# Reordering the first stages of a fused cross-attention kernel

## The chip, the cores and the metric

The kernel runs on one core of one Trainium2 chip. Its engines work side by side, each through a queue of its own in the order of the program: TensorE (PE, matrix products, with PEld for the loading of its weights), VectorE (DVE), ScalarE (ACT), GpSimd (POOL) and SyncE (SP), whose queue issues nearly all transfers (DMAs). The metric is the device time of one execution in microseconds (us), lower is better. Everything is computed in float32.

## The reference

Eight batches of 112 rows `x` with 320 channels attend to contexts of 375 rows with 512 features. The last 4 context rows are "prompts"; the other 371 are text. There are 20 heads of 16 channels.

```python
q   = heads(hidden_states @ W_q)
k_t = heads(text_ehs @ W_k)
v_t = heads(text_ehs @ W_v)
probs_t  = softmax(einsum('bhsd,bhtd->bhst', q, k_t) * attn_scale)
text_out = einsum('bhst,bhtd->bhsd', probs_t, v_t)
k_ip, v_ip = heads(ip_ehs @ W_k_ip), heads(ip_ehs @ W_v_ip)
attn_scores = einsum('bhsd,bhnd->bhsn', q, k_ip) * attn_scale
qsem = l2norm(einsum('bhst,bte->bhse', probs_t, text_ehs))
sem  = einsum('bhse,bne->bhsn', qsem, l2norm(ip_ehs))
probs_ip = softmax(attn_scores + 0.5 * sem) * spatial_mask
out = (text_out + einsum('bhsn,bhnd->bhsd', probs_ip, v_ip)) @ W_out + b_out + hidden_states
```

## The kernel before

**The scheme.** The norm of `qsem` is taken without forming it: with the gram matrix G of the text rows, the squared norm is the sum of p (G p) over the text. Per batch the kernel builds a wide matrix `u`: the upper triangle of the gram (its diagonal blocks halved and everything doubled), the products of the text with the normalised prompts, a column of ones, and 16 value columns. One product of the turned, unnormalised probabilities with `u` then gives, for each head, the row for the norm, the prompts' similarities, the sum of the softmax and the text output (line 770, tile `ps_qd`).

**Staging.** A batch has 5 groups of 4 heads. The main loop runs over steps (batch, group). A step multiplies its group by `u` in 12 blocks of 32 text rows, computes scores, maxima (VectorE, line 721) and exponentials (ScalarE, line 735) of the group two steps ahead (`LEAD = 2`), sends these probabilities by DMA into a tile `xg` (line 742), where VectorE turns them (line 751, `turned`), and at its end runs pieces of the next batches' preparation (`between`): gram, values, keys, queries, and the turning of the context of the batch after next on VectorE (line 428, three pieces a batch). The order of PE, VectorE, SP and, in the loop, ScalarE is the order of the program text; the first stages, up to `prologue.close()`, are in program order on every engine.

**The first stages** (lines 1157 to 1203). Batch 0's context comes in three chunks of up to 128 rows, turned by PE (`transposed_context`, line 438) and copied out by ScalarE (first and third chunk) and VectorE (second). `awake(n)` multiplies the identity by itself to keep PE busy. `first_gram` yields after each of six products (line 476): chunk 1 by itself, chunks 1 and 2 with chunk 2, all three with chunk 3. `normalised_prompts` scales the prompts (square root on ScalarE, line 278) and turns both the scaled and the unscaled ones on PE (line 288). ScalarE doubles the gram into `ug` (line 492), GpSimd halves the diagonal blocks (line 493). `gram_to_groups` (line 538) copies `ug` into `u` by DMA: 4 blocks of 32 rows, each to 4 groups of 32 partitions, 16 transfers. Then follow queries (line 369, three chunks; scaled by VectorE, line 378, and copied by ScalarE, line 382), keys (line 562), the scores of the first two groups, values (line 596), and their regrouping and placing into `u` (lines 616 and 668). `spread` (line 143) rearranges columns of the weights on GpSimd.

**Banks.** PE's outputs outside the main product and the scores rotate through two banks (`ps_mm`, from `bank()`); the scores rotate through two others (`ps_sc`), which `bank(..., spare=True)` takes as well. A product waits until the bank's last contents have been read.

**Loads.** SP issues in program order: batch 0's context, a part of `x`, the weights of queries, keys and values, batch 1's context; then `ug` to `u` and the probabilities as they come; behind the first stages the two prompt weights (`load_embed`), and at the end of the first step the whole of batch 2's context (`load_next`, eight transfers). In steps, `run(("c", nb + 1), ...)` turns one third of the next context but one: for batch 2 at groups 1 and 2 of batch 0 and in group 4.

Of the kernel before, what the change touches and what calls it, by code (L numbers as in the profile page):

```python
# [8 lines left out]
F32 = mybir.dt.float32  # L9
AF = mybir.ActivationFunctionType  # L10
ALU = mybir.AluOpType
# [9 lines left out]
def kernel(  # L21
# [14 lines left out]
    nc = tc.nc  # L36
# [131 lines left out]
            )  # L168

    def load_ctx(b):  # L170
        if b > 0:
            load_ctx_blocks(b)
            return loaded[b]
        ct = io.tile([P, NT, E], F32, tag="ct", name=f"ct_{b}")
        for c in range(NT):
            rows = min(P, T - c * P)
            some = rows - rows % 16
            nc.sync.dma_start(ct[:some, c, :], ehs[b, c * P : c * P + some, :])
            if some < rows:
                nc.sync.dma_start(ct[some:rows, c, :], ehs[b, c * P + some : c * P + rows, :])  # L180
        return ct
# [13 lines left out]
    load_pairs(nc.sync, wq_sb, w_q)  # L195
    load_embed(nc.sync, wk_sb, w_k)
    load_embed(nc.sync, wv_in, w_v)
    loaded[1] = load_ctx(1)
    load_x_blocks(1, 0)

    half = const.tile([P, NT, P], F32, tag="half", name="half")
# [65 lines left out]

    def normalised_prompts():

        sq = work.tile([N, E], F32, tag="ipn", name="ipsq", bufs=1)  # L270
        ss = small.tile([N, 1], F32, tag="ipss", name="ipss", bufs=1)
        nc.vector.tensor_tensor_reduce(
            out=sq, in0=ip_sb, in1=ip_sb, scale=1.0, scalar=0.0, op0=ALU.mult, op1=ALU.add,
            accum_out=ss,
        )
        nc.vector.tensor_scalar_max(ss, ss, EPS * EPS)
        rn = small.tile([N, 1], F32, tag="iprn", name="iprn", bufs=1)
        nc.scalar.activation(rn, ss, AF.Sqrt)
        nc.vector.reciprocal(rn, rn)

        ipn = work.tile([N, E], F32, tag="ipn", name="ipn", bufs=1)
        nc.vector.tensor_scalar(ipn, ip_sb, rn, 0.5, op0=ALU.mult, op1=ALU.mult)
        yield

        for src, dst, n in ((ipn, ipnT, "n"), (ip_sb, ipT, "r")):
            ps = bank(f"ps_ipT{n}")
            for e in range(NE):
                nc.tensor.transpose(
                    ps[:, e * N : (e + 1) * N], chunk(src, e), ident[:N, :N]
                )  # L290
            nc.vector.tensor_copy(
                dst, ps[:, : NE * N].rearrange("p (e n) -> p e n", n=N)
            )
        yield

    def prompt_projections():
# [87 lines left out]


    st = {}

    def load_next(b):
        if 2 <= b < B:
            loaded[b] = load_ctx(b)  # L390

    def begin(b):
        s = st[b] = dict(ct=loaded.pop(b))
# [140 lines left out]
    def gram_to_groups(b, blocks, eng=nc.sync, parts=range(GROUP)):  # L534

        for q in blocks:
            for a in parts:
# [2 lines left out]
                    ug[q * RG : (q + 1) * RG, :],  # L540
                )

    def keys(b):
        s = st[b]
        if b > 0:
            nc.gpsimd.tensor_copy(s["kT"][:, :, TT:], kip[:, :, b * NIP : (b + 1) * NIP])
        for i in range(NC):
            ps = bank(f"ps_k_{b}_{i}", spare=0 < b < B - 1 and i == FULL)
            if 0 < b < B - 1 and i == FULL:

                for c in range(NT):
                    rows = min(P, TT - c * P)
                    nc.tensor.transpose(  # L553
                        ps[:, c * P : c * P + rows],
                        s["k3"][:rows, c].rearrange("p a r d -> p (a r d)"),
                        ident[:rows, :rows],
                    )
                nc.scalar.copy(s["kT"][:, i, :TT], ps[:, :TT])
                yield
                return  # L560
            for e in range(NE):
                nc.tensor.matmul(  # L562
                    ps[:, :TT],
                    wk_sb[:, e, i * P : (i + 1) * P],
                    s["ctxT"][:, e, :TT],
                    start=(e == 0),
                    stop=(e == NE - 1),
                )
            nc.scalar.copy(s["kT"][:, i, :TT], ps[:, :TT])
            yield  # L570
# [537 lines left out]
    def between(b, g):  # L1108
# [28 lines left out]
        if g == 3:  # L1137
# [3 lines left out]
                run(("f", b - 1), None)  # L1141
            for bs in rest:
                run(("q", bs[0]), None)
        if nb + 1 < B and g in ((1, 2) if b == 0 else (0, 1, 2)):
            run(("c", nb + 1), lambda: transposed_context(nb + 1))
        for bs in first:
            if g in ((0, 1) if b == 0 else (2, 3)[: len(bs)]):
# [10 lines left out]
    prompts = normalised_prompts()  # L1158
    context = transposed_context(0)
    products = first_gram()  # L1160
    next(prompts)
    awake(4)
    next(context)
    awake(3)
    next(context)
    next(products)
    next(prompts)
    next(context)
    run(("q", 0), lambda: project_queries(pairs[0]))
    drain(products)  # L1170
    nc.scalar.preload_act_table(AF.Exp)
    gram_to_groups(0, range(QN // 2))
    run(("q", 0), None)
    order_values()
    run(("k", 0), lambda: keys(0))
# [1 line left out]
    for a in range(GROUP):  # L1177
        scores(0, 0, a, early=True)
        probabilities(0, 0, a)
    gram_to_groups(0, range(QN // 2, QN))  # L1180
    spread(nc.gpsimd, wq_sb)
    nc.gpsimd.tensor_copy(wv_sb[:, :, C:], wk_sb[:, :, FULL * P : C])
    spread(nc.gpsimd, wk_sb)
# [2 lines left out]
    for a in range(GROUP):  # L1186
        scores(0, 1, a, early=True)
        probabilities(0, 1, a)
    run(("v", 0), None)
    drain(turned(0, 0, BLK))  # L1190
    for some in ([(a, a) for a in range(GROUP)], *across[1:]):
        regrouped(0, nc.gpsimd.tensor_copy, some)
    regrouped(0, nc.scalar.copy, across[0])
    placed(0, 0)
    run(("k", 0), None)
    run(("q", 0), None)
    load_x_blocks(2, 1)
    load_embed(nc.sync, wkip_sb, w_k_ip)
    load_embed(nc.sync, wvip_sb, w_v_ip)
    run(("k", 0), None)  # L1200
    run(("v", 1), lambda: values(1))
    more_constants()
# [36 lines left out]
    for n, (b, g) in enumerate(steps[:-NG]):  # L1239
# [11 lines left out]
        for j, _ in enumerate(multiplied(b, g)):  # L1251
            if j == 0:
# [10 lines left out]
                    probabilities(*c, a, hold=True)  # L1263
                if n == NG - 1:
                    run(("c", LEAD), None)
            if j == 5:
                for c, a in then:
                    scores(*c, a)
# [28 lines left out]
        if g == 0 and b > 1:  # L1297
            run(("f", b - 2), None)
        load_rest(n)
        if n == 0:  # L1300
            load_next(2)
        if g in ctx_blocks and b < B - 3:
            load_ctx_blocks(b + 3, ctx_blocks[g])
        for c, i in x_loads.get((b, g), ())[1:]:
# [162 lines left out]
```

## Time and profile before

| | |
|---|---|
| median of 3 runs | 416.43 us (415.19 to 416.9) |
| the profiled execution | 415.67 us, of which 414.0 us are the span of its instructions |
| busy: PE / VectorE / ScalarE / GpSimd | 98% / 82% / 52% / 31% of the span |
| granted TensorE clock, mean | 1.00 |
| start of the first main product | 35.4 us |
| DMA, share of 16 engines | 51.6% for the main queue |

In rows of instructions in order of time the first number is the start in us from the start of the span, the second the time to the end of the last of the group, and `xN` the number of instructions put together; in square brackets stands how long the engine was idle before and what ended that. One float32 product of a chunk is two passes on PE. In the list of waits the columns are: total us, times, longest. In the chain of waits each row is one piece of the chain that ended last.

### The profile page before, as it was taken

What the parts mean: (1) busy time and instruction counts of PE and PEld (TensorE: products, weight loads), DVE (VectorE), ACT (ScalarE), POOL (GpSimd) and SP (SyncE); (2) the same over time, 40 slices, a digit from 0 to 9 for tenths busy, and PEclk for the clock granted to TensorE, in tenths of its full rate; (3) what the DMA queues carried; (4) which work ended last, traced back from release to release, by engine and by line L of the source; (5) the groups of instructions that cost most, each with busy time, mean ns of one, the idle gap of its engine ahead of it and who ended that gap; (6) DMA issues with size and microseconds to landing.
All of it is one profiled execution on the core that took longest, in us unless ns stands there. A gap on an engine that the chain in (4) does not pass through costs nothing.

```text
span 414.0 us, 14122 instructions
## 1 busy us (share of the span) xinstructions
PE 406.8 (98%) x5490; PEld 319.8 (77%) x5490; DVE 338.0 (82%) x731; ACT 217.0 (52%) x729; POOL 126.7 (31%) x314
## 2 busy tenths in 40 slices
PE   8999999999999999999999999999999999999995
PEld 7766778797777867788677877788777987787893
DVE  4455489988899979889799988888798977889784
ACT  2543234636365453745357363653637563688773
POOL 5442121112081212612054120702117120545540
PEclk9999999999999999999999999999999999999999
DMA  6766856556655455455554555546444356544300
GB/s 186 193 164 177 191 142 154 154 149 163 176 143 149 140 144 142 107 144 167 129 138 127 145 150 137 152 107 180 123 126 114 96 169 159 129 123 132 108 2 29
DMA packets 46723, 57.56 MB, mean 139 GB/s; under 512 B 9501, under 2 KB 41057, under 8 KB 46656
## 3 DMA queue, kind: packets, MB, share of 16 engines
q1 hardware_dynamic: 46616, 56.60, 51.6%
q8 instruction: 43, 0.70, 0.7%
q14 instruction: 24, 0.20, 0.2%
q10 hardware_dynamic: 40, 0.07, 0.1%
HBM read 15.88 MB, written 1.39 MB: 42 GB/s over the span
## 4 chain that ended last, share of the span: by engine, by line
PE 93%; DVE 3%; DMA 2%; ACT 1%; issue 0%; SPq 0%; DVEq 0%
PE ps_qd L770 41%; PE ps_v L596 14%; PE ps_s L699 11%; PE ps_k L562 10%; PE ps_g L520 7%; PE ps_q L369 3%; PE ps_o L987 3%; PE ps_g L476 1%; DMA ct<-in_ctx_dram 1%; DVE xgT L751 1%; DMA xg<-p 1%; PE ps_k L578 1%; PE ps_k L553 1%; ACT p L735 1%; PE ps_a L975 0%
## 5 line engine op out<-in xcount | busy, mean ns | idle before, releaser
L770 PE MATMUL ps_qd<-u,xgT 32*112 32x168 f32 (+11 forms) x3840 | 217.2, 350 | 0.0
L770 PEld LDWEIGHTS ps_qd<-u,xgT 32*112 32x112 f32 x3840 | 185.6, 172 | 25.1 <-issue 0.7
L751 DVE STREAM_TRANSPOSE xgT<-xg 128x512 f32<-128x512 f32 (+2 forms) x79 | 125.9, 1601 | 7.1 <-DMA xg<-p 5.1
L735 ACT ACTIVATE p<-ps_s,nmx 112x371 f32<-112x371 f32 x156 | 84.5, 579 | 86.7 <-DVE nmx L721 81.6
L721 DVE TENSOR_REDUCE nmx<-ps_s 112x1 f32<-112x371 f32 x160 | 78.4, 535 | 26.8 <-PE ps_s L699 22.0
L816 DVE CUSTOM_DVE_ANT_0 junk<-ps_qd,p 112x371 f32<-112x371 f32 x146 | 79.2, 543 | 19.8 <-ACT pvs L783 4.2
L668 POOL COPY u<-vr 128x64 f32<-128x64 f32 x120 | 26.5, 239 | 134.3 <-PE ps_qd L770 102.2
L699 PE MATMUL ps_s<-kT,qm 32*112 32x375 f32 (+1 forms) x320 | 65.9, 495 | 0.0
L596 PE MATMUL ps_v<-wv_sb,ctxT 128*128 128x384 f32 (+1 forms) x192 | 63.3, 479 | 0.8 <-ACT qT L382 0.8
L596 PEld LDWEIGHTS ps_v<-wv_sb,ctxT 128*128 128x128 f32 x192 | 35.6, 190 | 23.1 <-ACT qT L382 1.4
L562 PE MATMUL ps_k<-ctxT,wk_sb 128*128 128x371 f32 x136 | 46.7, 486 | 0.0
L699 PEld LDWEIGHTS ps_s<-kT,qm 32*112 32x112 f32 x320 | 25.8, 171 | 12.2 <-issue 10.2
L616 ACT COPY vr<-vext 32x240 f32<-32x240 f32 x88 | 34.2, 389 | 1.3
L562 PEld LDWEIGHTS ps_k<-ctxT,wk_sb 128*128 128x128 f32 x136 | 24.5, 189 | 13.4
L603 ACT COPY vext<-ps_v 128x384 f32<-128x384 f32 (+1 forms) x24 | 11.2, 467 | 39.7 <-PE ps_v L596 39.7
L520 PE MATMUL ps_g<-ctxT 128*32 128x375 f32 (+11 forms) x672 | 30.4, 333 | 0.0
L520 PEld LDWEIGHTS ps_g<-ctxT 128*32 128x32 f32 x672 | 27.7, 110 | 2.0
L737 ACT COPY ipl<-ps_s 112x4 f32<-112x4 f32 x140 | 23.1, 165 | 0.0
L428 DVE STREAM_TRANSPOSE ctxT<-ct 128x512 f32<-128x512 f32 x21 | 23.0, 1106 | 0.0
L962 POOL TENSOR_TENSOR wv<-vip,w 112x1280 f32<-112x1280 f32 x6 | 14.8, 2468 | 26.7 <-DVE w L899 26.7
L492 ACT ACTIVATE ug<-ps_g 128x375 f32<-128x375 f32 (+2 forms) x24 | 8.3, 375 | 25.5 <-issue 12.0
L493 POOL TENSOR_TENSOR ug<-ug,half 128x128 f32<-128x128 f32 (+1 forms) x24 | 10.5, 449 | 29.2 <-ACT ug L492 29.2
(169 smaller groups left out, 337.4 us busy)
## 6 DMA issues: line engine op xcount, KB each, us to landing
xg<-p SPq DMA_DIRECT2D x156, 162.3 KB
u<-ug SPq DMA_DIRECT2D x128, 99.0 KB
ct<-in_ctx_dram SPq DMA_DIRECT2D x28, 176.0 KB
vip<-vipd SPq DMA_DIRECT2D x6, 560.0 KB
xr_sb<-in_x_dram SPq DMA_DIRECT2D x32, 35.0 KB
out_dram<-ob SPq DMA_DIRECT2D x8, 140.0 KB
x_sb<-in_x_dram SPq DMA_DIRECT2D x6, 140.0 KB
xg<-wv_sb SPq DMA_DIRECT2D x4, 162.3 KB
```

Source lines behind the costliest of these rows:

```text
L520: nc.tensor.matmul(ps[c][q * RG : (q + 1) * RG, j * RG - c * P : T - c * P], ctxT[:, e, j * RG : (j + 1) * RG], ctxT[:, e, j * RG : T], st ...
L562: nc.tensor.matmul(ps[:, :TT], wk_sb[:, e, i * P : (i + 1) * P], s["ctxT"][:, e, :TT], start=(e == 0), stop=(e == NE - 1),)
L596: nc.tensor.matmul(ps[:, :w], ctxT[:, e, c * P : (c + 1) * P], wv_sb[:, e, :w], start=(e == 0), stop=(e == NE - 1),)
L616: copy(s["vr"][a * RG : (a + 1) * RG, q::QN].rearrange("p c g d -> p c (g d)"), s["vext"][q * RG : (q + 1) * RG, :, a * w : (a + 1) * w],)
L668: nc.gpsimd.tensor_copy(v, dealt(b, c, s["vr"][:, c * QN : (c + 1) * QN, g, :]))
L699: nc.tensor.matmul(ps[:S, :w], qm[a * RG : (a + 1) * RG, i, r, j * S : (j + 1) * S], s["kT"][a * RG : (a + 1) * RG, i, :w], start=True, st ...
L721: nc.vector.tensor_reduce(nmx, s["sc", g, a][:S, :TT], AX.X, ALU.max, negate=True)
L735: nc.scalar.activation(s["p", g][:, a, :], ps[:S, :TT], AF.Exp, bias=nmx)
L737: nc.scalar.copy(s["ipl"][:, groups[g][a], :], ps[:S, TT:T])
L751: nc.vector.transpose(xT[:, j0:j1].rearrange("p j (k q) -> p q j k", q=QN), xg[:, :, j0 * RG : j1 * RG].rearrange("p q (j k) -> p q j k", ...
L770: nc.tensor.matmul(banks[a][:S, j * RG : UW], xT[a * RG : (a + 1) * RG, j, :S], region(b, c)[a * RG : (a + 1) * RG, q, j * RG - c * P :], ...
L816: nc.vector.tensor_tensor_reduce(out=junk, in0=ps[:S, :TT], in1=s["p", g][:, a, :], scale=1.0, scalar=0.0, op0=ALU.mult, op1=ALU.add, accu ...
```

## The change

- The first gram piece comes ahead of the second context chunk's turn, the third chunk right after the second, and 2 instead of 3 identity products ahead of them.
- The prompts are turned once, by a product with a 32 x 64 matrix: the identity beside a diagonal of 0.5 over the norm. It gives unscaled and scaled prompts in one bank. The scaling is moved from the 32 x 512 prompts to the 32 x 32 diagonal.
- `grams_in_place`: GpSimd copies, for each block q, the rows that stay on the same partitions (32 x 792). By DMA go the other 12 of 16: block 0 to three groups first, the nine others after the first group's probabilities.
- The third query chunk goes ahead of the second and third key chunks, and ahead of the turn of the first group's probabilities.
- The prompts' value weights are loaded in the first step instead of ahead of it. Batch 2's context is loaded in two halves, at the ends of the first and second step, and its turns are at groups 2 and 3 instead of 1 and 2 (the last in group 4 as before).
- Batch 1's third key chunk takes a bank of `ps_mm` instead of `ps_sc`.

```diff
@@ first stages: loads
-    loaded[1] = load_ctx(1)
+    load_ctx_blocks(1)
@@ def normalised_prompts():
+        both = small.tile([N, 2 * N], F32, tag="ipid", name="ipid", bufs=1)
+        nc.vector.tensor_copy(both[:, :N], ident[:N, :N])
...
-        ipn = work.tile([N, E], F32, tag="ipn", name="ipn", bufs=1)
-        nc.vector.tensor_scalar(ipn, ip_sb, rn, 0.5, op0=ALU.mult, op1=ALU.mult)
-        yield
-
-        for src, dst, n in ((ipn, ipnT, "n"), (ip_sb, ipT, "r")):
-            ps = bank(f"ps_ipT{n}")
-            for e in range(NE):
-                nc.tensor.transpose(
-                    ps[:, e * N : (e + 1) * N], chunk(src, e), ident[:N, :N]
-                )
-            nc.vector.tensor_copy(
-                dst, ps[:, : NE * N].rearrange("p (e n) -> p e n", n=N)
-            )
+        nc.vector.tensor_scalar(both[:, N:], ident[:N, :N], rn, 0.5, op0=ALU.mult, op1=ALU.mult)
+        yield
+
+        ps = bank("ps_ipT")
+        for e in range(NE):
+            nc.tensor.matmul(
+                ps[:, e * 2 * N : (e + 1) * 2 * N], chunk(ip_sb, e), both, start=True, stop=True
+            )
+        v = ps[:, : NE * 2 * N].rearrange("p (e k n) -> p k e n", k=2, n=N)
+        nc.vector.tensor_copy(ipnT, v[:, 1])
+        nc.vector.tensor_copy(ipT, v[:, 0])
         yield
@@
+    def grams_in_place(b):
+
+        for q in range(QN):
+            some = slice(q * RG, (q + 1) * RG)
+            nc.gpsimd.tensor_copy(st[b]["u"][some, q * GW : (q + 1) * GW], ug[some, :])
+
@@ def keys(b):
-            ps = bank(f"ps_k_{b}_{i}", spare=0 < b < B - 1 and i == FULL)
+            ps = bank(f"ps_k_{b}_{i}", spare=1 < b < B - 1 and i == FULL)
@@ def between(b, g):
-        if nb + 1 < B and g in ((1, 2) if b == 0 else (0, 1, 2)):
+        if nb + 1 < B and g in ((2, 3) if b == 0 else (0, 1, 2)):
@@ the first stages
-    next(prompts)
     awake(4)
     next(context)
-    awake(3)
+    next(prompts)
+    awake(2)
+    next(products)
     next(context)
-    next(products)
+    next(context)
     next(prompts)
-    next(context)
     run(("q", 0), lambda: project_queries(pairs[0]))
     drain(products)
     nc.scalar.preload_act_table(AF.Exp)
-    gram_to_groups(0, range(QN // 2))
+    grams_in_place(0)
+    gram_to_groups(0, (0,), parts=range(1, GROUP))
...
-    gram_to_groups(0, range(QN // 2, QN))
+    for q in range(1, QN):
+        gram_to_groups(0, (q,), parts=[a for a in range(GROUP) if a != q])
...
     run(("v", 0), None)
+    run(("q", 0), None)
     drain(turned(0, 0, BLK))
...
     run(("k", 0), None)
-    run(("q", 0), None)
     load_x_blocks(2, 1)
     load_embed(nc.sync, wkip_sb, w_k_ip)
-    load_embed(nc.sync, wvip_sb, w_v_ip)
@@ the main loop
+            if n == 0 and j == 2:
+                load_embed(nc.sync, wvip_sb, w_v_ip)
...
-        if n == 0:
-            load_next(2)
+        if n < 2:
+            load_ctx_blocks(2, halves[n])
```

More of the change, by code (lines that the diff above doesn't have):

```diff
@@ L386 @@
     st = {}
-    def load_next(b):
-        if 2 <= b < B:
-            loaded[b] = load_ctx(b)
     def begin(b):
```

3 lines of the change are left out of this document (removed).

## The prediction

> **What bounds the kernel now.** I read the page's engine table first, then the list of TensorE's waits, then the instructions in order of time for the stages that the change touches.
>
> ```profile
> PE 406.8 (98%) x5490; PEld 319.8 (77%) x5490; DVE 338.0 (82%) x731; ACT 217.0 (52%) x729; POOL 126.7 (31%) x314
> ```
>
> TensorE (PE) is busy for 406.8 of 414.0 us. Where it has work it is the bound, so an edit gains only what it takes from PE's work or PE's waits. This is the whole list of waits of 0.5 us or more:
>
> ```profile
> PE ps_w L455 <- POOL ident masks.py:199: 1.5, 1, 1.5
> PE ps_v L596 <- ACT qT L382: 0.8, 1, 0.8
> PE ps_wT L1074 <- DVE w_last L1069: 0.8, 1, 0.8
> PE ps_k L553 <- ACT ipl L737: 0.5, 1, 0.5
> ```
>
> The first and third lie outside the change. It touches the second (0.8 us, at the first chunk of batch 1's values) and the fourth (0.5 us, at batch 1's third key chunk). With the work before the first gram, that is all there is to win. Gains in transfers that arrive earlier behind a busy PE count nothing.
>
> **The change part by part.** (a) *The opening.* PE in order of time:
>
> ```profile
> 1.47 2.08 PE L455 MATMUL ps_w<-ident 128*128 128x128 f32 x8 [1.47 <-POOL ident masks.py:199]
> 3.56 1.13 PE L438 MATMUL ps_c<-ident,ct 128*128 128x128 f32 x4
> 4.48 0.89 PE L455 MATMUL ps_w<-ident 128*128 128x128 f32 x6
> 5.54 0.75 PE L438 MATMUL ps_c<-ident,ct 128*128 128x128 f32 x4 [0.17 <-DMA ct<-in_ctx_dram]
> 6.21 1.16 PE L476 MATMUL ps_g<-ctxT 128*128 128x128 f32 x8
> 7.30 0.66 PE L288 MATMUL ps_ipTn<-ident,ipn 32*128 32x32 f32 x4
> 7.81 0.64 PE L288 MATMUL ps_ipTr<-ident,ip_sb 32*128 32x32 f32 x4
> 8.38 0.74 PE L438 MATMUL ps_c<-ident,ct 115*128 115x115 f32 x4
> 8.95 4.63 PE L476 MATMUL ps_g<-ctxT 128*128 128x128 f32 x40
> 13.42 0.83 PE L369 MATMUL ps_q<-xT,wq_sb 128*128 128x112 f32 x6
> ```
>
> Start to start, the costs are 0.67 us for the second chunk's turn, 1.09 for the first gram piece, 0.51 + 0.57 for the prompts' two turns, 0.57 for the third chunk, 4.47 for the other 40 passes. From 5.54 PE never rests, so the queries start at 13.42. The six idle-filling passes at 4.48 become four, and the first gram piece goes ahead of the second chunk, into time in which PE now waits for data. It needs the first chunk copied out by ScalarE:
>
> ```profile
> 2.14 1.28 ACT L278 ACT_TABLE_LOAD   x1 [2.14 <-issue]
> 5.60 0.56 ACT L448 COPY ctxT<-ps_c 128x512 f32<-128x512 f32 x1
> 5.73 0.15 DVE L279 RECIPROCAL iprn<-iprn 32x1 f32<-32x1 f32 x1 [0.27 <-ACT iprn L278]
> 6.32 0.69 DVE L446 COPY ctxT<-ps_c 128x512 f32<-128x512 f32 x1
> ```
>
> Today that copy stands behind the square root of the prompts. Afterwards it comes first, as soon as the turn that started at 3.56 ends (4.69): done at 5.25, and the gram piece starts at about 5.3. Then: second chunk 6.4, third 7.1, ready for the prompts at 7.65. The program's order shows a price: a second table load of ScalarE between copy and square root, 1.28 us: 5.25 + 1.28 = 6.5, root and reciprocal and one small VectorE operation to about 7.1, still early enough. But the prompts' product takes the bank of the second chunk, which VectorE frees 0.69 us after about 7.2: 7.9, a wait of 0.25. The product has eight passes; at 4.47/40 = 0.11 each that is 0.9, against 1.08 for the two turns. No row shows this form: the bounds are 0.45 (half the passes of the gram at its pace) and 1.08 (eight at the 0.135 of the old turns); 0.9, the gram's pace, is nearest in kind. End: 7.9 + 0.9 + 4.47 = 13.3, against 13.42. **Gain 0.1** (bounds: 0.6 gained, 0.1 lost).
>
> (b) *Some of the first grams' rows by GpSimd.* Of 16 DMAs u<-ug 4 become GpSimd copies; of the rest three instead of eight stand ahead of the first probabilities on SP. Rows of the stage:
>
> ```profile
> 15.27 0.40 POOL L1182 COPY wv_sb<-wk_sb 128x256 f32<-128x256 f32 x1
> 17.68 5.09 SPq L538 DMA_DIRECT2D u<-ug  x8
> 22.86 3.72 SPq L742 DMA_DIRECT2D xg<-p  x4
> 23.19 0.20 POOL L505 COPY ctxT<-ipnT 128x16 f32<-128x16 f32 x1 [6.11 <-DVE ctxT L428]
> 25.75 2.66 PE L562 MATMUL ps_k<-ctxT,wk_sb 128*128 128x371 f32 x8
> 26.05 0.44 ACT L603 COPY vext<-ps_v 128x320 f32<-128x320 f32 x1
> 28.24 0.82 PE L369 MATMUL ps_q<-xT,wq_sb 128*128 128x112 f32 x6
> 29.05 1.17 PE L562 MATMUL ps_k<-ctxT,wk_sb 128*128 128x371 f32 x3
> 29.17 2.95 DVE L751 STREAM_TRANSPOSE xgT<-xg 128x1536 f32<-128x1536 f32 x1 [3.63 <-DMA xg<-p]
> 31.96 0.28 DVE L378 TENSOR_SCALAR qm<-ps_q,emask 128x112 f32<-128x112 f32 x1
> 32.27 0.25 ACT L382 COPY qT<-ps_q 128x112 f32<-128x112 f32 x1 [3.36 <-DVE qm L378]
> 32.58 2.85 PE L596 MATMUL ps_v<-wv_sb,ctxT 128*128 128x384 f32 x8 [0.79 <-ACT qT L382]
> 33.67 0.58 POOL L668 COPY u<-vr 128x64 f32<-128x64 f32 x3 [2.08 <-DMA u<-ug]
> ```
>
> An issue of u<-ug takes 5.09/8 = 0.64 us, so the probabilities leave SP at about 19.6 instead of 22.86, and the last u<-ug is out by 19.6 + 3.72 + 9 x 0.64 = 29.1 instead of 26.58 + 8 x 0.64 = 31.7. The transfer's 3.63 us and most of the 2.08 us of GpSimd's wait go, but PE works on keys meanwhile: worth nothing by itself. Price on GpSimd: 4 copies of 792 columns; at most 0.40 x 792/256 = 1.24 each, together 5.0, against its 6.11 us of idle before 23.19. The spreading of the weights' columns behind them is wanted by the queries' third chunk only (28.24, afterwards about 25.6) and is done by some 22. **Cost 0**; without that cover it would hold PE by what it exceeds.
>
> (c) *Queries ahead of keys.* Today the third query chunk's scaling (31.96) stands on VectorE behind the turn (29.17, 2.95 us), ScalarE's copy waits for it, and PE's first value chunk of batch 1 waits for their bank: 0.79 us. Afterwards the queries come right after the last values, and the scaling stands ahead of the turn. PE: 25.65 queries, 26.45 key chunk 1 (whose bank ScalarE frees at 26.05 + 0.44 = 26.49 today, hence no or 0.05 us of waiting), 28.95 key chunk 2, 31.45 values. Banks: key chunk 2 wants the query bank, free by some 27; values want that of key chunk 1, copied out by about 29.6. So the 0.79 goes. The ends of passes are modelled: key chunk 1 takes 28.24 - 25.75 = 2.49 from start to start, and the second's first pass at 29.05 + 2.49 is 31.54, by which the stall was 1.04. **Gain 0.9**, between the two. Late next is GpSimd's placing (33.67): in the new order done by 32, PE wants it at about 34.2.
>
> (d) *Second half of batch 2's context one group later, its turns at groups 2 and 3, batch 1's third key chunk in another bank.* Two kinds of load move past each other on SP: four of the eight context loads go behind group 1's probabilities, the prompts' value weights behind two probability transfers. SP is ahead by then (b), and no row shows PE waiting for these. But VectorE's turn of 1.05 us moves from group 1 to group 3, ahead of the maxima of batch 1's second group. The chain of waits there, with two rows of the engines:
>
> ```profile
> 76.30 0.81 DVE L378 TENSOR_SCALAR qm<-ps_q,emask 128x224 f32<-128x224 f32 x2 [0.25 <-PE ps_q L369]
> 78.10 1.05 DVE ctxT L428
> 79.14 1.25 DVE xgT L751
> 81.44 0.57 ACT p L735
> 82.12 0.54 PE ps_k L553 x3
> 82.73 0.54 ACT L558 COPY kT<-ps_k 128x371 f32<-128x371 f32 x1
> 83.81 0.51 PE ps_ip L678 x6
> ```
>
> VectorE is without a gap from 76.30 to past 82, so the extra 1.05 moves everything behind it. The exponentials come at 82.5, and ScalarE's copy of the key chunk, third behind them in its queue, at 83.8 to 84.3. The 0.5 us wait before the key chunk goes (its bank is no longer one of the scores'), but the new bank is one of two that rotate: key chunk, queries, prompt logits. The logits need the bank of the key chunk, so they wait for that copy: 84.3 instead of 83.81. **Loss 0.5** in place of the gain of 0.5; bounds: gain 0.5, loss 1.05. At the next step VectorE has idle time and the delay runs out.
>
> Sum: -0.1 - 0.9 + 0.5 = -0.5 us. The profiled execution took 415.67 us (span 414.0 and 1.67 around it): 415.2. The median of the runs, 416.43, lies 0.76 above it; by the median I forecast **415.9 us**.
>
> [...] One microsecond of the opening by windows (PE, weight loads, VectorE, ScalarE, GpSimd, clock):
>
> ```profile
> 2.00:3.00 1.00, 1.00 (x7) 1.00 (x6) 0.97 (x2) 0.86 (x1) 0.94 (x5) 1.00 0.86 266
> ```
>
> The passes of the identity at 1.47 cost 2.08/8 = 0.26 each, those at 4.48 0.89/6 = 0.15: PE became fast by 4.5, before the passes that are removed. [...]
>
> **The rivals.** *A: VectorE's move costs nothing*, if the loads or PE's lead leave it room in group 3: both waits go, -0.1 - 0.9 - 0.5 = -1.5: 414.9. Against it: the only idle time in the row is 0.25. *B: slower.* VectorE's 1.05 is not made up in the next step; the second pair of scores there waits for exponentials as well and PE loses up to 1.05 once more: +0.55, 417.0. It decides once the delay left at that point passes some 0.1 us more than PE's own 0.5. *C: slow clock in the opening.* The first gram piece runs at 0.26/0.15 of its price: 1.09 becomes 1.9, and the sum -0.5 + 0.8 = +0.3: 416.7. *D: the query bank is not the wait.* If another bank or the earlier stage takes the 0.9, what stays is -0.1 + 0.5: 416.8.
>
> **How the numbers follow.** Forecast 0.45, A 0.29, B 0.13, C 0.05, D 0.08. About 0.5% (2.1 us) is what a measurement of this kernel can tell from no change: its three runs spread by 1.7 us. All five cases lie within it; with that spread and the bounds (at best -0.6 - 1.04 - 0.5 = -2.1; at worst, with D and the bound of (d), 0.1 + 1.05 = +1.15) I give faster 0.15, same 0.77, slower 0.08. The range 414.4 to 417.2 takes in A and B with part of the runs' spread.
>
> **What the next profile would show.** (a) the first gram piece at about 5.3, a second table load behind ScalarE's first copy, the queries at 13.3; if later than 13.5, (a) is wrong. (b) first probabilities issued from about 19.6; GpSimd's four copies done before 20. (c) no wait of PE before batch 1's first values, which start near 31.4. (d) no wait at the third key chunk, one of about 1 us at the prompt logits for ScalarE's key copy; if the logits don't wait, A holds. Wrong altogether if PE's list shows a wait of over 0.5 us anywhere else: for a context load in group 2, or at the second scores of group 4.

## The result and the profile after

The changed kernel takes **417.13 us** (median of 22 runs, 416.49 to 419.69), the kernel before 415.99 us in 22 runs of the same comparison (414.71 to 417.3). The ratio is 1.0042 with a 95% interval of 1.0026 to 1.0057: slower by 0.4%, where 0.1% faster was forecast (415.9 us). It lies inside the bound of 0.5% and at the upper end of the range (417.2), but on the other side of the kernel before than was forecast.

One thing is needed to read the median: the executions of the changed kernel fall into two groups, 14 of the 22 at 416.49 to 417.24 us and 8 at 418.63 to 419.69. The kernel before has no such gap. The profiled execution, 417.11 us with a span of 415.4, is of the lower group.

The engine table of the changed kernel, and its list of TensorE's waits:

```profile
PE 408.4 (98%) x5488; PEld 319.8 (77%) x5488; DVE 340.5 (82%) x732; ACT 218.5 (53%) x730; POOL 129.7 (31%) x318
```

```profile
PE ps_w L448 <- POOL ident masks.py:199: 1.5, 1, 1.5
PE ps_wT L1073 <- DVE w_last L1068: 1.1, 1, 1.1
PE ps_ip L677 <- ACT kT L557: 0.5, 1, 0.5
PE ps_ipT L285 <- DVE ctxT L439: 0.3, 1, 0.3
```

PE is busy for 1.6 us more with two instructions fewer. The two waits that the change touches (0.8 and 0.5) are gone, one of 0.5 at the prompt logits is new, and so is one of 0.3 ahead of the prompts' product. More busy time without more work points at passes that have become slower. PE in order of time, in the opening and at the first scores of the main loop:

```profile
5.34 1.39 PE L469 MATMUL ps_g<-ctxT 128*128 128x128 f32 x8
...
7.99 2.08 PE L285 MATMUL ps_ipT<-ipid,ip_sb 32*128 32x64 f32 x8 [0.32 <-DVE ctxT L439]
9.99 4.72 PE L469 MATMUL ps_g<-ctxT 128*128 128x128 f32 x40
14.55 0.83 PE L366 MATMUL ps_q<-xT,wq_sb 128*128 128x112 f32 x6
...
32.77 2.74 PE L595 MATMUL ps_v<-wv_sb,ctxT 128*128 128x384 f32 x8
35.45 0.57 PE L698 MATMUL ps_s<-kT,qm 32*112 32x371 f32 x2
...
84.17 0.76 PE L677 MATMUL ps_ip<-kipb,qT 128*112 128x32 f32 x6 [0.54 <-ACT kT L557]
84.86 0.57 PE L698 MATMUL ps_s<-kT,qm 32*112 32x375 f32 x2
```

The same two points in the kernel before, main loop's start and batch 1's start:

```profile
35.36 0.57 PE L699 MATMUL ps_s<-kT,qm 32*112 32x371 f32 x2
...
84.24 0.57 PE L699 MATMUL ps_s<-kT,qm 32*112 32x375 f32 x2
```

Read as a ledger, the time goes like this. The first queries start 1.13 us later than before (14.55 against 13.42): that is the opening, and most of it is the prompts' product, 2.00 us from start to start for eight passes, 0.25 each, where the two turns took 1.08. How large this difference is depends on the execution. PE's first passes follow each other at 0.21 us, until they become fast (0.11). In the kernel before the queries start at 13.42 where that comes at 4.6 us, as in this profile, and at 14.28 where it comes at 7.7 ("The queries alone" below). The changed opening gains nothing by an early moment: 14.55 at 5.9 us here, and 14.57 at 4.8 in the run with batch 2's context as before. So the 1.13 is that of an early execution, and in late ones it may be less. The main loop begins only 0.09 later (35.45 against 35.36), so the queries ahead of the keys won 1.04 us. At the start of batch 1 the delay is 0.62 (84.86 against 84.24): the wait for ScalarE's key copy and what goes with it cost 0.53. Another 0.2 comes in the step after that (below), and the last 0.5 in the tail, where one small VectorE operation on PE's path took 0.65 us in place of 0.18. VectorE in the tail of the changed kernel, and below it of the kernel before:

```profile
401.05 0.65 DVE L870 TENSOR_TENSOR rn<-ss,z 112x16 f32<-112x16 f32 x1 [0.15 <-ACT shared L808]
```

```profile
400.22 0.18 DVE L871 TENSOR_TENSOR rn<-ss,z 112x16 f32<-112x16 f32 x1
```

This operation isn't touched by the change. In a second profile of the same kernel (the repeat, below) the wait that follows it is 0.8 us, as before, so it belongs to single executions; what causes it stayed open. Without it the sum is 0.1 + 0.5 + 0.2 = 0.8 us, and the middle run of the lower group, 416.77, lies 0.8 above the median of before. That the two agree so well is in part luck, as the opening of the one profile of before is an early one.

What the forecast saw and did not see of VectorE's move, in rows of VectorE, ScalarE and the weight loads of the changed kernel:

```profile
77.01 1.08 DVE L421 STREAM_TRANSPOSE ctxT<-ct 128x512 f32<-128x512 f32 x1
...
82.29 0.57 ACT L734 ACTIVATE p<-ps_s,nmx 112x371 f32<-112x371 f32 x1 [0.97 <-DVE nmx L720]
83.58 0.54 ACT L557 COPY kT<-ps_k 128x371 f32<-128x371 f32 x1
...
85.55 0.27 PEld L769 LDWEIGHTS ps_qd<-u,xgT 32*112 32x112 f32 x2 [0.40 <-DVE ss L815]
```

and the weight loads of the kernel before at the same place:

```profile
84.71 0.43 PEld L770 LDWEIGHTS ps_qd<-u,xgT 32*112 32x112 f32 x2 [0.18 <-DVE ss L816]
```

The turn runs at 77.01, ScalarE's exponentials wait 0.97 us for the maxima behind it, the key copy follows at 83.58, and the prompt logits wait for it. Besides, the next step's products need banks that VectorE's reductions (`ss`) free, and these come later too: 0.40 us at the first block where it was 0.18.

### The profile page after: what moved, and what is told of

It reads as the page before. It is cut to its first block, busy times and chain, and to the rows that moved or that the text cites. A ratio compares the mean times of both kernels' runs of the same rounds, so it can differ in the third digit from the quotient of the medians.

```text
span 415.4 us, 14117 instructions
## 1 busy us (share of the span) xinstructions
PE 408.4 (98%) x5488; PEld 319.8 (77%) x5488; DVE 340.5 (82%) x732; ACT 218.5 (53%) x730; POOL 129.7 (31%) x318
## 4 chain that ended last, share of the span: by engine, by line
PE 93%; DVE 4%; ACT 1%; issue 1%; POOL 0%; DVEq 0%; POOLq 0%
PE ps_qd L769 39%; PE ps_v L595 15%; PE ps_k L561 11%; PE ps_s L698 10%; PE ps_g L513 7%; PE ps_q L366 3%; PE ps_o L986 3%; PE ps_g L469 1%; DVE junk L815 1%; PE ps_k L577 1%; PE ps_ipT L285 1%; PE ps_w L448 0%; PE ps_a L974 0%; PE ps_k L552 0%; DVE nmx L720 0%
```

## The experiments

Two theories of the slow product stood at the start. The first goes by its weights: `chunk(ip_sb, e)` takes every fourth element of a row, so neighbours in the weights are 16 bytes apart, and reading them is slow. The second (K) goes by the clock: PE's clock falls, because two identity passes and their place were given up. Beside these stood the parts (c) and (d) of the prediction, each to be tried alone. The repeats and the comparisons each have their own runs of the kernel before beside them.

**The prompts turned twice, as before.** In the changed kernel `normalised_prompts` gets its old body back; all else stays.

```diff
-        both = small.tile([N, 2 * N], F32, tag="ipid", name="ipid", bufs=1)
...
-                ps[:, e * 2 * N : (e + 1) * 2 * N], chunk(ip_sb, e), both, start=True, stop=True
+        for src, dst, n in ((ipn, ipnT, "n"), (ip_sb, ipT, "r")):
+            ps = bank(f"ps_ipT{n}")
+            for e in range(NE):
+                nc.tensor.transpose(ps[:, e * N : (e + 1) * N], chunk(src, e), ident[:N, :N])
```

> The changed kernel with one thing undone: the prompts are scaled and turned twice on PE as in the kernel before, at the new place. In the changed kernel the single product took 2.08 us for its eight passes (7.99 to 9.99, 0.25 each) where I had priced 0.9. Theory F (the form of the product is slow, whatever the clock): the two turns cost about 1.1 us as before, the queries start at about 13.6 instead of 14.55, and the whole is about 1.0 us faster than the changed kernel, level with the kernel before or up to 0.3 us faster. Theory K (PE's clock is slow there because fewer identity products ran ahead): the turns take about 2 us too and nothing is gained.

Measured: 416.43 us (416.08 to 417.15, 11 runs) against 416.19 before, ratio 1.0 [0.9988, 1.0012]; no second group. PE in order of time:

```profile
8.30 0.66 PE L285 MATMUL ps_ipTn<-ident,ipn 32*128 32x32 f32 x4 [0.71 <-DVE ctxT L439]
8.80 0.64 PE L285 MATMUL ps_ipTr<-ident,ip_sb 32*128 32x32 f32 x4
9.37 4.72 PE L469 MATMUL ps_g<-ctxT 128*128 128x128 f32 x40
13.93 0.83 PE L366 MATMUL ps_q<-xT,wq_sb 128*128 128x112 f32 x6
```

The two turns take 1.07 us in place of 2.00, and the queries start 0.62 earlier than in the changed kernel. The other 0.3 goes into a longer wait for the bank (0.71 against 0.32), since the scaling of 32 x 512 prompts again stands on VectorE ahead of the copy that frees it. So the one product is what made the opening longer, but undoing it alone doesn't bring the opening of before back. The median is 0.7 us under that of the changed kernel, where 1.0 was expected.

**The same product with its weights side by side.** GpSimd copies the prompts into a tile in which each chunk's columns are neighbours.

```diff
+        ipc = small.tile([N, NE, P], F32, tag="ipc", name="ipc", bufs=1)
+        nc.gpsimd.tensor_copy(ipc, ip_sb.rearrange("t (p e) -> t e p", e=NE))
...
-                ps[:, e * 2 * N : (e + 1) * 2 * N], chunk(ip_sb, e), both, start=True, stop=True
+                ps[:, e * 2 * N : (e + 1) * 2 * N], ipc[:, e, :], both, start=True, stop=True
```

> The changed kernel, with the prompts first copied by GpSimd into an order in which the 128 weights of a pass lie side by side (in the changed kernel they lie 16 bytes apart); the product itself is the same. Theory F1 (the stride of the weights makes the passes slow): the eight passes take about 0.9 us, 0.11 each, and the queries start about 1.1 us earlier than 14.55. Theory F2 (a 32-row product of this kind is slow in itself): 0.25 a pass as before, no gain. Theory K (clock): no gain either.

Measured: 416.21 us (415.68 to 417.2, 12 runs), ratio 0.9995 [0.9983, 1.0008]; no second group. The product's line in three kernels, as the view of one line gives it (shortest / median / longest in ns). The kernel before, whose turns read the same strided rows:

```profile
L288 PEld LDWEIGHTS ps_ipTr<-ident,ip_sb x4: 214/214/214, 7.8 to 8.1; 32*128 32x128 f32 x4
```

the changed kernel:

```profile
L285 PEld LDWEIGHTS ps_ipT<-ipid,ip_sb x8: 303/324/327, 8.0 to 9.6; 32*128 32x128 f32 x8
```

and with the weights side by side, the line and its place in time:

```profile
L287 PEld LDWEIGHTS ps_ipT<-ipid,ipc x8: 181/187/187, 8.2 to 9.0; 32*128 32x128 f32 x8
```

```profile
8.25 1.07 PE L287 MATMUL ps_ipT<-ipid,ipc 32*128 32x64 f32 x8 [0.41 <-POOL ct L156]
13.81 0.83 PE L368 MATMUL ps_q<-xT,wq_sb 128*128 128x112 f32 x6
```

The same eight passes load their weights in 187 ns in place of 324 and take 1.0 us in place of 2.0. The moving operand, the count and the place are the same, so the layout of the weights is the cause. The queries come 0.74 us earlier than in the changed kernel, not the 1.1 expected: in this execution PE becomes fast at 6.2 us in place of 5.9, and the product starts 0.26 later (8.25 against 7.99). Its wait is named after a GpSimd operation that ends at 8.11; VectorE's copy of the second chunk, which frees the bank, ends at 8.10.

That the two turns load the same strided rows in 214 ns, where the product takes 324, no run here takes apart.

**The product issued twice.** The same result, computed once more into the same bank, to price a pass and to see what the clock does. (Of the 22 executions of the changed kernel 8 are long, not the 7 that the expectation counts.)

```diff
-            for e in range(NE):
+            for e in (*range(NE), *range(NE)):
```

> The changed kernel with the prompts' product (weights 16 bytes apart) issued twice, with the same result: 16 passes instead of 8. It measures two things. The price of a pass: 0.25 us each by the trace, so 2.0 us more. And a second effect: of 22 executions of the changed kernel 7 took 418.6 to 419.7 us and the others 416.5 to 417.3, as did 5 of 12 of the kernel with the context loads put back, but none of 23 with the prompts turned twice or with weights side by side. Theory Q (slow passes leave PE so little busy that its clock falls back for some microseconds, depending on when they come): with 4 us of them most or all executions pay the 2 us as well: about 421 us. Rival (the two groups come from something else): one third at about 421, two thirds at 419.

Measured: 421.08 us (420.48 to 422.84, 5 runs) against 415.88 before, ratio 1.0136 [1.0113, 1.0158]. PE in time, and windows of one microsecond (window, length, busy time and count of PE, weight loads, VectorE, ScalarE and GpSimd, granted clock, DMA share, GB/s):

```profile
8.25 3.99 PE L285 MATMUL ps_ipT<-ipid,ip_sb 32*128 32x64 f32 x16 [0.32 <-DVE ctxT L439]
12.17 6.86 PE L469 MATMUL ps_g<-ctxT 128*128 128x128 f32 x40
18.87 0.83 PE L366 MATMUL ps_q<-xT,wq_sb 128*128 128x112 f32 x6
```

```profile
9.00:10.00 1.00, 1.00 (x6) 1.00 (x6) 0.00 (x0) 0.00 (x0) 0.00 (x0) 0.92 1.00 379
10.00:11.00 1.00, 1.00 (x6) 1.00 (x5) 0.00 (x0) 0.00 (x0) 0.00 (x0) 0.50 1.07 410
...
13.00:14.00 1.00, 1.00 (x6) 1.00 (x6) 0.41 (x2) 0.00 (x0) 1.00 (x1) 0.50 1.19 234
...
16.00:17.00 1.00, 1.00 (x8) 1.00 (x8) 0.00 (x0) 0.00 (x0) 0.00 (x0) 0.66 0.33 74
17.00:18.00 1.00, 1.00 (x12) 1.00 (x11) 0.00 (x0) 0.48 (x1) 0.15 (x1) 1.00 0.34 60
```

Eight more passes cost 1.9 us of their own. They cost the same at a granted clock of 0.92 as at 0.50 (six in a microsecond), and each still loads its weights in 325 ns. But the run lost 5.2 us against before, where the 0.8 of the changed kernel's lower group and these 1.9 make 2.7: the clock fell to 0.50 at 9.85 us (0.92 in the window from 9 to 10), while PE was working through the slow passes without a gap, came back within the window from 16 to 17 (0.66), and the 40 passes of the gram took 6.70 us from start to start (4.56 in the changed kernel). These 2.1 us are most of the rest. In the windows, a gram pass at 13 to 14 takes twice what it takes at 17 to 18 (6 against 12 in a microsecond). The reason that theory Q gives, a PE that is little busy, no run shows: in these windows, from 9 us on, its busy share is 1.00.

**More identity passes.** K says that the clock should hold with more of them.

```diff
-    awake(2)
+    awake(4)
```

> The changed kernel with four identity products instead of two between the first chunk's turn and the first gram piece. Theory K of the rivals (fewer identity products leave the clock low for longer): the first gram piece and the product run faster, and the whole gains 0.5 us or more over 417.1. Theory F1 (the stride costs the passes their time): no gain; the first gram piece starts up to 0.5 us later, and the whole is the same or up to 0.5 us slower.

Measured: 418.57 us (417.12 to 420.3, 6 runs), ratio 1.0064 [1.0041, 1.0088]. PE in time, and one window:

```profile
6.23 1.56 PE L469 MATMUL ps_g<-ctxT 128*128 128x128 f32 x8
9.05 2.12 PE L285 MATMUL ps_ipT<-ipid,ip_sb 32*128 32x64 f32 x8 [0.32 <-DVE ctxT L439]
11.11 6.15 PE L469 MATMUL ps_g<-ctxT 128*128 128x128 f32 x40
17.09 0.83 PE L366 MATMUL ps_q<-xT,wq_sb 128*128 128x112 f32 x6
```

```profile
12.00:13.00 1.00, 1.00 (x7) 1.00 (x7) 0.35 (x2) 0.00 (x0) 1.00 (x1) 0.50 1.16 239
```

K falls: with four more passes (the first gram piece comes 0.9 us later) the product is as slow as it was, and the clock fell to 0.50 all the same, at 10.70 (0.85 in the window from 10 to 11), before the product's end. The median is 1.4 us above that of the changed kernel, more than either theory gave: 0.9 for the passes, and long executions on top. This profiled execution, 419.66 us, lies where the changed kernel's second group lies, though 0.9 of it are the extra passes. Its gram takes 5.98 us in place of 4.56, so what the fall of the clock is seen to cost is 1.4 us of the 2.4 between the groups.

No profile of the changed kernel itself fell into its second group, so that the fall of the clock makes that group is an inference from four things. They are this profile, the one of the doubled product, the absence of the group in the two kernels above that lack the slow passes (0 of 11 and 0 of 12 runs), and the mean granted clock, which is on record for every run. In the three series with the product issued once as the change has it (the changed kernel, its repeat, and the next kernel below) 15 of the 18 long runs show 0.992 to 0.995 and three 0.996; none of the 26 short ones shows less than 0.996. In the short one that was profiled, what is missing to 1.000 comes after PE's last pass, which ends at 411.8 us: from 412 on the clock reads 0.50. Two comparisons below speak against taking a fall of the clock behind slow passes for the only way to a long execution. Kernels without slow passes were long too: two of 12 runs of one (420.04 and 422.06, at 0.993 and 0.989), and one of 12 of another (418.54, at 0.999).

Why only some executions are long, no trace shows. In both profiles with a fall it came 3.4 us after PE's passes had become fast (6.43 and 9.85; 7.29 and 10.70), and lasted 6.8 and 3.4 us. In that stretch the only gap of PE in either list of waits is the one of 0.32 us ahead of the product. Where the passes became fast at 4.8, 5.9 and 6.1 us, the slow product was followed by no fall (granted clock 1.00 from 8 to 16 us). That a late start of the fast passes brings the fall about is a guess of the author from these five profiles. Turns and a wait ahead of the product do not do it by themselves: the kernel with weights side by side became fast at 6.2 us, had 1.5 us of them (6.74 to 8.25) and no slow gram behind them (4.56 us), and the doubled product had 1.4. A late start of the fast passes also moves the product itself, to 8.25 us at 6.43, which may be a part of the other 1.0 us of the second group.

**Batch 2's context as before.** Part (d) undone, the key chunk's new bank kept.

```diff
-        if n < 2:
-            load_ctx_blocks(2, halves[n])
+        if n == 0:
+            load_ctx_blocks(2)
...
-        if nb + 1 < B and g in ((2, 3) if b == 0 else (0, 1, 2)):
+        if nb + 1 < B and g in ((1, 2) if b == 0 else (0, 1, 2)):
```

> The changed kernel with batch 2's context loaded at the end of the first step and turned at groups 1 and 2 as in the kernel before; the third key chunk of batch 1 keeps its new bank. Theory of the prediction (VectorE's turn of 1.05 us, moved into group 3, delays the exponentials and the key copy): the prompt logits' wait of 0.5 us goes, batch 1's first main product starts at about 84.2 instead of 84.9, and the step behind it gains another 0.2: 0.6 to 0.9 us faster than the changed kernel. Rival (the bank alone makes the logits wait): the wait stays and the time is the same. Rival (loads in one piece hold up a turn of probabilities): a new wait in groups 1 or 2.

Measured: 416.01 us (415.63 to 418.07, 12 runs), ratio 1.0004 [0.9987, 1.0021]; the two groups are there (7 runs up to 416.06, 5 from 417.61), as the slow product is. PE in time:

```profile
83.31 0.76 PE L677 MATMUL ps_ip<-kipb,qT 128*112 128x32 f32 x6
84.00 0.57 PE L698 MATMUL ps_s<-kT,qm 32*112 32x375 f32 x2
```

The logits no longer wait, nor does the key chunk, and batch 1 starts at 84.00 in place of 84.86. So the new bank does remove the old wait, and the move of the context's turn is what puts one in its place. The lower group, 415.84 in the middle, is 0.9 us below that of the changed kernel, at the upper end of what was expected. The move costs nothing more behind batch 1's start: the next step begins at 94.36 here and at 95.23 in the changed kernel, 0.87 apart where it was 0.86. But the gain of the new bank does not last. Against the kernel before, batch 1 starts 0.24 earlier (84.00 for 84.24) and the next step only 0.03 (94.36 for 94.39), since the first blocks wait 0.40 us for VectorE's reductions here too, against 0.18 before. PE comes there earlier, VectorE doesn't.

**The queries alone.** The kernel before with one line moved.

```diff
     run(("v", 0), None)
+    run(("q", 0), None)
     drain(turned(0, 0, BLK))
...
     run(("k", 0), None)
-    run(("q", 0), None)
```

> The kernel before with one part of the change: the third query chunk ahead of the second and third key chunks. Theory of the prediction: the wait of 0.79 us before batch 1's first values goes; the first main product starts 0.8 to 1.0 us earlier than 35.4 and the whole is that much faster than the kernel before (ratio about 0.998). Rival (the transfer of the probabilities or of the grams' rows, which this kernel leaves late, takes the wait's place): the placing of values in u, at 33.7 in the kernel before, holds the first main product, and the gain is under 0.5 us.

Measured: 415.51 us (414.66 to 418.54, 12 runs) against 416.19, ratio 0.9982 [0.9965, 0.9998]. PE in time:

```profile
4.54 1.49 PE L455 MATMUL ps_w<-ident 128*128 128x128 f32 x6
14.28 0.83 PE L369 MATMUL ps_q<-xT,wq_sb 128*128 128x112 f32 x6
35.17 0.57 PE L699 MATMUL ps_s<-kT,qm 32*112 32x371 f32 x2
```

The wait of 0.79 is gone. From the first queries to the first scores it is 20.89 us, as in the changed kernel (35.45 - 14.55 = 20.90), against 21.94 before: 1.05 us won, and (b) is not in this kernel. Of this the medians show 0.7. The profile tells where the rest can go: the opening is here the code of before, yet its identity passes at 4.54 cost 0.25 each where the profile of before has 0.15, and the queries start 0.86 later. PE's passes become fast at 7.7 us here and at 4.6 there. The opening has a spread of nearly 1 us from one execution to another, by that moment.

**The mended kernel.** Prompts side by side (with a bank of the scores for the product, so that it needn't wait for the second chunk's copy, and the square root's table loaded ahead of ScalarE's first copy) and batch 2's context as before. The rest of the change stays.

```diff
+    nc.scalar.preload_act_table(AF.Sqrt)
...
+        ipc = small.tile([N, NE, P], F32, tag="ipc", name="ipc", bufs=1)
+        nc.gpsimd.tensor_copy(ipc, ip_sb.rearrange("t (p e) -> t e p", e=NE))
...
-        ps = bank("ps_ipT")
+        ps = bank("ps_ipT", spare=True)
...
-        if nb + 1 < B and g in ((2, 3) if b == 0 else (0, 1, 2)):
+        if nb + 1 < B and g in ((1, 2) if b == 0 else (0, 1, 2)):
...
-        if n < 2:
-            load_ctx_blocks(2, halves[n])
+        if n == 0:
+            load_ctx_blocks(2)
```

> The changed kernel with what the first runs pointed to: weights side by side for the prompts' product (GpSimd copies them), batch 2's context loaded and turned as in the kernel before, and two small edits: the product's output goes to a bank of the scores, so it needn't wait for the second chunk's copy, and the table for the square root is loaded at the start, so that no second load stands between. Expected from the sum: product 0.9 to 1.1 us instead of 2.1, no wait at the prompt logits, no wait of 0.3 ahead of the product: 1.0 + 0.85 + 0.3 = 2.1 us under the changed kernel's 417.1, that is 415.0, about 0.27% faster than the kernel before. Rival (the three parts cover each other, or something else comes to the front in the opening): 415.5 to 416.2.

Measured: **414.43 us** (414.16 to 414.55, 5 runs) against 415.88, ratio 0.9963 [0.9949, 0.9976]. PE's waits and PE in time:

```profile
PE ps_w L451 <- POOL ident masks.py:199: 1.5, 1, 1.5
PE ps_wT L1076 <- DVE w_last L1071: 0.7, 1, 0.7
```

```profile
7.28 1.10 PE L288 MATMUL ps_ipT<-ipid,ipc 32*128 32x64 f32 x8
12.87 0.83 PE L369 MATMUL ps_q<-xT,wq_sb 128*128 128x112 f32 x6
33.95 0.57 PE L701 MATMUL ps_s<-kT,qm 32*112 32x371 f32 x2
82.48 0.57 PE L701 MATMUL ps_s<-kT,qm 32*112 32x375 f32 x2
```

Only the first and the last wait are left. The queries start at 12.87, the main loop 1.4 us and batch 1 1.8 us earlier than before. What each of the four edits gives of this was not tried apart. The kernel beats both others, at 0.6 us below the 415.0 expected, and its repeat in a later comparison says the same:

> The mended kernel again. If its gain of 0.37% over the kernel before (414.4 us) is one of the kernel and not of those five executions, it stays at 414.3 to 415.0 with no second group.

Measured: 414.74 us (414.46 to 415.1, 8 runs) against 416.26, ratio 0.9969 [0.9956, 0.9983]. All 13 runs of the two comparisons lie below the fastest of the changed kernel, 416.49. In the profile of the repeat PE becomes fast later (6.7 us in place of 5.2), and the queries start at 13.60.

**The mended kernel with all 16 block copies by DMA.** What part (b) is worth.

```diff
-    grams_in_place(0)
-    gram_to_groups(0, (0,), parts=range(1, GROUP))
+    gram_to_groups(0, range(QN // 2))
...
-    for q in range(1, QN):
-        gram_to_groups(0, (q,), parts=[a for a in range(GROUP) if a != q])
+    gram_to_groups(0, range(QN // 2, QN))
```

> The kernel b1_mended with all 16 copies of the first gram's rows into u by DMA again, in the old order. Theory of the prediction (GpSimd's part is worth nothing by itself, as PE works on keys meanwhile): the same time as b1_mended within 0.3 us, and no new wait of PE. Rival: with PE 2 us earlier in the opening the last rows come too late for the placing, and the first main product waits: 0.5 to 1.5 us slower than b1_mended.

Measured: 415.96 us (414.91 to 422.06, 12 runs), ratio 1.0014 [0.9992, 1.0036], taken without the run at 422.06. PE in time, as profiled in this comparison:

```profile
14.10 0.83 PE L369 MATMUL ps_q<-xT,wq_sb 128*128 128x112 f32 x6
34.98 0.57 PE L701 MATMUL ps_s<-kT,qm 32*112 32x371 f32 x2
```

From the queries to the first scores it takes 20.88 us, against 21.08 and, in the repeat, 20.89 with GpSimd's copies, and no wait of PE is added. So the profiles give (b) nothing. The median was 1.5 us worse all the same (1.3 without the longest run), with single runs at 420.04 and 422.06, at mean granted clocks of 0.993 and 0.989, that nothing here explains. The repeat:

> The mended kernel with all 16 copies by DMA, again. Its first times spread from 414.9 to 422.1, and its profile shows no wait that the mended kernel lacks, only a slower clock in the opening. If GpSimd's rows are worth nothing (prediction), its lower times stand within 0.3 us of the mended kernel's. Rival: they cost or save something of their own, and it stays 0.5 us or more above.

Measured: 415.2 us (414.12 to 416.66, 12 runs), ratio 0.9977 [0.9961, 0.9992]; without such runs. Its interval overlaps that of the mended kernel. What (b) is worth stays open, between nothing and some 0.5 us by this second comparison; no wait of PE shows it. What the expectation calls a slower clock are passes 0.21 us apart up to 7.8 us; over such passes the granted clock reads 1.00 in the profiles of the kernel before (2 to 4 us) and of the changed kernel (2 to 5 us).

**The changed kernel once more**, beside the last two:

> The changed kernel again, on the same chip and in the same rounds as the two kernels below. If the clock falls back in part of its executions (theory Q: with the product twice the 40 gram passes behind it took 6.7 us instead of 4.6), its times again stand in two groups some 2 us apart, 416.5 to 417.3 and 418.6 to 419.7; if its profile falls into the upper group, the gram passes behind the product take 6 us or more.

Measured: 418.13 us (416.54 to 419.66, 10 runs) against 416.26, ratio 1.0045 [1.0024, 1.0066]. Both groups are there again, 5 runs up to 417.4 and 5 from 418.86. The median moved by 1 us between two comparisons only because the share of the second group did; the ratio's interval is nearly the same.

## Why the prediction was wrong

The sum of -0.5 failed at one term, the price of the prompts' product in (a). The others held, but two were missing: a small wait in (d), and the long executions.

- **(a) The opening: wrong, and this decides the sign.** The step that failed is "eight passes at 4.47/40 = 0.11 each that is 0.9", with the bounds 0.45 and 1.08. Measured: 2.00 us. The price was taken from the gram, the nearest row by kind of operation, whose weights lie side by side. The rows that share the layout, the old turns' 0.135 a pass, did not show the cost either, since a turn loads these weights in 214 ns where the plain product takes 324. No row showed a plain product with strided weights, and the upper bound should have said so. The rest of (a) came as forecast: the gram piece at 5.34 (5.3), the second table load between copy and root, a wait of 0.32 (0.25). The queries were forecast for 13.3 and came at 14.55; 1.1 of these 1.25 us is this term, and the product's start (7.99 for 7.9) and the gram's 40 passes (4.56 for 4.47) gave 0.1 each. The 13.42 that the forecast starts from was itself an early one, as the 14.28 of the same opening in another execution shows.

ScalarE's second table load in the changed kernel:

```profile
5.31 1.28 ACT L277 ACT_TABLE_LOAD   x1
```

- **The clock: probably a second way in which the slow passes cost.** In 8 of 22 runs, and in 5 of 10 of the repeat, the kernel loses some 2.4 us more; that the clock does it is inferred, as said above, and 1.4 us of it are seen in a profile. Rival C had a slow clock too, but in the first gram piece. That identity passes given up make the clock fall (K) no run shows: with four more of them it fell to 0.50 as well. The first gram piece is slow in some executions: it took 1.23 us in the changed kernel's profile where 1.09 was priced (at a granted clock of 1.00), and 1.87 in a profile of the mended kernel with all copies by DMA, in which PE became fast at 7.8 us. But it takes 1.49 in the opening of the kernel before, too (7.7 us). So "PE became fast by 4.5" was read from one early execution and is no property of the kernel. What C gave, 416.7, is near the result by accident.
- **(b) GpSimd's rows: right that PE does not notice.** The four copies took 0.92 us each, below the bound of 1.24, and were done by 19.3; the first probabilities left at 20.56, 1.0 later than forecast as everything behind the opening was. GpSimd and SP's queue in order of time:

```profile
15.59 3.69 POOL L540 COPY u<-ug 32x792 f32<-32x792 f32 x4
20.56 3.70 SPq L741 DMA_DIRECT2D xg<-p  x4
```

- **(c) Queries ahead of keys: right.** The wait went (the values start at 32.77 without one; 31.4 was forecast, and the late opening, 14.55 for 13.3, is nearly all of the difference), and the gain was 1.04 by starts, the upper of the two figures between which 0.9 was taken. The line alone was worth 0.7 us in medians.
- **(d) The context's turn: right in mechanism, and in size at batch 1's start.** The key chunk's wait went and the logits wait for ScalarE's key copy; batch 1 lost 0.53. The wait is 0.54 in the list, where the signs gave about 1. Rival A (it costs nothing) and D (the query bank isn't the wait) fall. Missing were the 0.2 that the next step's blocks wait for VectorE's reductions. This is not rival B, whose delay runs on behind the move of the turn: with the turn back in its old place the 0.2 are there as well. It is a part of the bank's gain that is lost again, so the bank is worth some 0.1 at the next step and not 0.5, and the move costs 0.87.

In all: forecast -0.1 - 0.9 + 0.5; found +1.1 - 1.0 + 0.5 + 0.2, which is 0.8 for the lower group, and the second group lifts the median to 1.1.

## What to carry to other kernels

Where two operations are folded into one, price the new one by a row with the same operands' layout, not only the same engine and shape; if there is none, the upper bound must be wide. Weights 16 bytes apart cost the float32 product here twice the time of weights side by side (2.00 against 1.00 us for eight passes), and a copy on an engine off the path bought that back. A stretch of slow passes in the opening may cost twice, once by itself and once by the clock behind it (in two profiles here 0.50 was granted behind it, and the gram took 1.4 and 2.1 us longer), so look at the spread of the runs and not at one profile before calling such a stage priced. And when two profiles are compared in the first microseconds, find out in each when PE becomes fast (here between 4.6 and 7.8 us).

## What the runs showed that was not expected

- The float32 product of 32 rows whose weights lie 16 bytes apart took 0.25 us a pass, at a granted clock of 0.50 (product issued twice) as at 1.00 (changed kernel); with weights side by side it took 0.125. The turns with the same stride took 0.135 (kernel before, 1.08 us for eight).
- The granted clock fell to 0.50 while PE was working through such passes without a gap, 3.4 us after PE had become fast, and came back 3.4 us later in one profile (eight slow passes) and 6.8 us later in another (sixteen). In three other profiles eight slow passes were followed by no fall; as far as the groups of times tell, it comes in a third to a half of the executions.
- The start of the kernel is not the same from one execution to the next. PE's passes become fast, 0.11 us from start to start in place of 0.21, between 4.6 and 7.8 us in the 13 profiles, at 4.6 and 7.7 with one and the same opening, and there it moves the first queries by 0.86 us. The recorded clock reads 1.00 from the start in both kernels' profiles.
